# Two graph attention layers on one core: each mask turned over by one transposing transfer instead of four

## The chip, the cores and the metric

The kernel runs on one core of a Trainium2 chip. The metric is the device time of one execution in microseconds (us); lower is better. The kernel before takes 3692.95 us, the median of 3 runs from 3692.69 to 3693.4. A core has five engines that each work through a queue of their own: TensorE (PE, with its weight loads PEld), VectorE (DVE), ScalarE (ACT), GpSimd (POOL) and SyncE (SP), which here only issues transfers (DMA).

## What is computed

There are 32 graphs ("images") of 512 nodes with 512 features each, in float32, and an integer adjacency matrix per graph. Two attention layers run one after the other, each with a residual:

```python
# layer 0: scores along the rows of the adjacency, softmax over the last axis
h = jnp.maximum(_layernorm(x, axis=-1), 0.0)
scores = leaky_relu(s_src[:, :, None] + s_dst[:, None, :] + attn_b[0], 0.2)
attn = softmax(where(adj + eye == 0, -inf, scores), axis=-1)
x = x + einsum('bij,bjh->bih', attn, h)
# layer 1: two GAT layers, the first with 4 heads of 256 features, the second with 1 head of 512
h = jnp.maximum(_layernorm(x, axis=-1), 0.0)
mask = (adj > 0) | eye
#   gat_layer: xl = x @ W ; e[s, d] = leaky_relu(asrc[s] + adst[d], 0.2)
#              attn = softmax(where(mask, e, NEG_INF), axis=1) ; out = einsum(attn, xl) + bias
h = elu(gat_layer(h, mask, W1, ..., concat=True))
x = x + gat_layer(h, mask, W2, ..., concat=False)
```

Each softmax needs the mask twice: along one axis, to find the largest score of every node before the exponent is taken, and along the other, to be added to the score matrix. The adjacency isn't symmetric, so each mask is needed as it lies and turned over.

## The kernel before

**Tiling.** The 512 nodes of an image are `T = 4` tiles of `P = 128` partitions. A mask is a bf16 buffer of 128 x 4 x 512: `m[p, t, n]` is the entry of node `t*128 + p` (row) and node `n` (column), 0 where there is an edge and a large negative number where there is none. `m0` is the mask of layer 0, `m1` that of layer 1; `m0T` and `m1T` are the same masks turned over. There is one buffer each for `m0`, `m0T` and `m1T`, and two for `m1`.

**How a mask is made.** `load_adj` (L663) loads the adjacency by a GpSimd transfer that also converts it. For `m0`, VectorE adds the identity to the four diagonal blocks (L680) and maps to 0 and `NO_EDGE` (L683); for `m1` it maps first (L695) and then clears the diagonal blocks (L701). Then `transposed_mask` (L665 to L671) issues four transposing transfers on SP, one for each `t`. Each turns the 128 x 512 slab `m[:, t, :]` and writes the 128 columns `t*128 ... t*128+127` of all four tiles of `mT`.

**Who reads the masks.** `edge_weights` (L582) makes the softmax weights `E` of one head:

- `a_row`, a score for each node, is brought to all partitions: `in_lines` writes the scores of a layer to a small DRAM buffer (L559), `row_of` reads one line of it into all 128 partitions (L569, by SP), and `in_bank` copies the line to PSUM on ACT (L579).
- four instructions on VectorE (L591) add mask and row and keep the maximum, one for each tile. They read `m0` in layer 0 and `m1T` in layer 1 (`mask_max`).
- L596 and L598 make the largest score of each node, and `spread` brings it to a PSUM bank, `m_bank`, by four transposes on PE (L487).
- for each tile: ACT makes the raw scores from `c_row` (L609), VectorE subtracts `m_bank` (L612), GpSimd adds the mask (L614; `m0T` in layer 0, `m1` in layer 1), ACT takes the exponent (L617).

PE then multiplies `E` with the node values (`aggregate`, L627). There are six such passes for an image: one in layer 0, four heads and the single head of the last layer (the kinds `E_one` and `E`). The other big user of PE is `products` (L822), the projections `x @ W1` and `x @ W2`. There are 24 L591 and 24 L614 in an image, of them 20 L591 on `m1T` and 4 L614 on `m0T`.

**What sets the order.** Nothing is issued as it is written down. Each call of `op(...)` gives a planner the engine that can do an instruction, its cost and the buffers that it reads and writes. `Plan.run` makes up to six drafts of the whole program. In a draft each engine always takes the waiting operation that is due first; the due times of the next draft are worked back from the one before, and the best draft is issued. For a transfer the costs are the time on the issuing queue, the time until it lands, and the time that it holds the DMA engines. If one cost is changed, the order of instructions on all engines can change, and it is then fixed: an engine that waits for one instruction doesn't go on to the next. The costs of a transposing transfer are 2200, 3000 and 600 ns. The same planner gives out the buffer places.

Some lines that the steps of the prediction name and that lie in other functions: L378 is a score product on VectorE (for the first image also the products that prepare the second layer's weights), L471 a sum of weights on GpSimd, L493 to L502 are the layer norm, L645 adds an attention's result to `x`.

Of the kernel before, what the change touches and what calls it, by code (L numbers as in the profile page):

```python
# [12 lines left out]
ALU = mybir.AluOpType  # L13
PSUM = bass.MemoryType.PSUM

P = 128
# [4 lines left out]
LOWEST = -3.0e38  # L21
# [21 lines left out]
class Plan:  # L43
# [15 lines left out]
    def op(self, engines, cost, emit, reads=(), writes=(), ahead=0, lock=None):  # L59

        i = len(self.ops)
        after = set()
        for buf, part in reads:
            after.update(buf.wrote.get(part, ()))
        for buf, part in writes:
            after.update(buf.wrote.get(part, ()))
            after.update(buf.read.get(part, ()))
        bufs = []  # L70
        for buf, part in (*reads, *writes):
            if buf.kind is not None and buf not in bufs:
                bufs.append(buf)
                if not buf.ops and buf.kind in self.turns:
                    self.turns[buf.kind].append(buf)
                buf.ops.append(i)
        for buf, part in reads:
            buf.read.setdefault(part, []).append(i)
        for buf, part in writes:
            buf.wrote[part] = [i]  # L80
            buf.read[part] = []
        after.discard(i)
        if not isinstance(engines, tuple):
            engines, cost, emit = (engines,), (cost,), (emit,)
        self.ops.append((engines, cost, emit, after, bufs, i - ahead, lock))
# [153 lines left out]
def on_dve(n, speed=1.0, scaled_psum=False):  # L239
    one = n / 0.96 / speed + (130.0 if scaled_psum else 70.0)  # L240
    return one, one + 85.0


def on_act(n, per_partition=0):

    one = n / 1.2 + (95.0, 140.0, 280.0)[per_partition]
    return one, one + 60.0


def on_pool(n, narrow=False):  # L250
    one = 2.04 * n + 70.0 if narrow else 2.2 * n + 100.0
    return one, one + 30.0
# [8 lines left out]
def kernel(  # L261
# [24 lines left out]
    nc = tc.nc  # L286
    B, N, D = x.shape
    H, F = att_src1.shape
    HF = H * F
    T = N // P  # L290
# [18 lines left out]
    def node_block(t: int) -> slice:  # L309
        return slice(t * P, (t + 1) * P)  # L310
# [31 lines left out]
    junk = big.tile([P, 512], BF16, name="junk")  # L342
# [4 lines left out]
    op = plan.op  # L347
# [135 lines left out]
    ROW = range(T)  # L483
# [48 lines left out]
    def spread(kind, part, col_of, ahead):  # L532

        row = Buffer(kind)
        for t in range(T):
            pe_transpose(
                ahead, row, lambda t=t: row.at[:, node_block(t)], part, lambda t=t: col_of(t).to_broadcast([P, P]), ident, t
            )
        return row
# [24 lines left out]
    def row_of(kind, lines, k):  # L564

        row = Buffer(kind)
        op(
            "SP", by_dma(4 * P * N, 4500.0),
            lambda: nc.sync.dma_start(  # L569
                row.at, bass.AP(tensor=lines.at.tensor, offset=lines.at.offset + k * N, ap=[[0, P], [1, N]])  # L570
            ),
            lines(0), row(*ROW), AHEAD,
        )
        return row

    def in_bank(kind, row):

        bank = Buffer(kind)
        op("ACT", on_act(N), lambda: nc.scalar.copy(bank.at, row.at), row(*ROW), bank(*ROW), AHEAD)  # L579
        return bank  # L580

    def edge_weights(kind, scores, ac, lines, k, mask_max, mask):  # L582


        a_of = lambda t: ac.at[:, k, t : t + 1]
        a_row = spread("a_bank", scores, a_of, AHEAD) if lines is None else in_bank("a_bank", row_of("a_row", lines, k))
        amax, z, m = Buffer("col"), Buffer("col"), Buffer("col")
        for t in range(T):
            op(
                "DVE", on_dve(N + 60),  # L590
                lambda t=t: nc.vector.tensor_tensor_reduce(  # L591
                    junk, mask_max.at[:, t, :], a_row.at, 1.0, LOWEST, ALU.add, ALU.max, accum_out=amax.at[:, t : t + 1]
                ),
                a_row(*ROW) + mask_max(*ROW), amax(t),
            )
        op("DVE", on_dve(T), lambda: nc.vector.tensor_add(z.at, ac.at[:, k + 1, :], amax.at), scores + amax(*ROW), z(0))  # L596
        op(
            "DVE", on_dve(T), lambda: nc.vector.scalar_tensor_tensor(m.at, z.at, SLOPE, z.at, op0=ALU.mult, op1=ALU.max),  # L598
            z(0), m(0),
        )  # L600

        E = Buffer(kind)
        m_row = spread("m_bank", m(0) + E("place"), lambda t: m.at[:, t : t + 1], AHEAD)
        c_of = lambda t: ac.at[:, k + 1, t : t + 1]
        c_row = spread("acc", scores + E("place"), c_of, AHEAD) if lines is None else row_of("c_row", lines, k + 1)
        for t in range(T):
            op(
                "ACT", on_act(N, 1),
                lambda t=t: nc.scalar.activation(E.at[:, t, :], c_row.at, AF.Prelu, bias=a_of(t), scale=1.0, alpha=SLOPE),  # L609
                c_row(*ROW) + scores, E(t),  # L610
            )
            op("DVE", on_dve(N), lambda t=t: nc.vector.tensor_sub(E.at[:, t, :], E.at[:, t, :], m_row.at), m_row(*ROW) + E(t), E(t))  # L612
            op(
                "POOL", on_pool(N, True), lambda t=t: nc.gpsimd.tensor_add(E.at[:, t, :], E.at[:, t, :], mask.at[:, t, :]),  # L614
                E(t) + mask(*ROW), E(t), lock=True,
            )
            op("ACT", on_act(N), lambda t=t: nc.scalar.activation(E.at[:, t, :], E.at[:, t, :], AF.Exp), E(t), E(t))  # L617
        return E
# [44 lines left out]
        op("POOL", (2200.0, 8000.0), lambda: nc.gpsimd.dma_start(m.at, node_tiles(adj, b)), (), m(*ROW))  # L663

    def transposed_mask(m, mT):  # L665
        for t in range(T):
            op(
                "SP", (2200.0, 3000.0, 600.0),
                lambda t=t: nc.sync.dma_start(mT.at[:, :, node_block(t)], m.at[:, t, :], transpose=True),
                m(t), mT(t),  # L670
            )  # L671

    def masks0(b):

# [33 lines left out]
    def layer0_scores(b):  # L708
        rstd, nmr = layernorm(X[b])
        h0, ac = Buffer("h"), Buffer("ac")  # L710
        for t in range(T):
            relu_normed(h0, X[b], t, rstd, nmr)
            for i, w in ((1, ws_r), (0, wd_r)):
                op(
                    "DVE", on_dve(D), lambda t=t, w=w, i=i: dot(h0.at[:, t, :D], w, ac.at[:, i, t : t + 1]),
                    h0(t) + W["w0"](0, 1), ac((i, t)), lock=True,
                )
        c = ac(*((1, t) for t in ROW))
        op(
            "DVE", on_dve(T), lambda: nc.vector.tensor_scalar(ac.at[:, 1, :], ac.at[:, 1, :], b0_r, None, op0=ALU.add),  # L720
            c + W["w0"](2), c,
        )
        m0, m0T = masks0(b)
        scores = c + ac(*((0, t) for t in ROW))

        L0[b] = (h0, edge_weights("E_one", scores, ac, in_lines(ac, scores, 2) if b else None, 0, m0, m0T))
# [144 lines left out]
    def layer1_scores(b, h):  # L871
        xl, j = L1[b][h // 2], h % 2
        m1, m1T = M[b]
        if j == 0:
            ac = gather(
                xl(*((i, t) for t in range(T) for i in range(2))),
                lambda: xl_of(xl)[:, :, :, :2].rearrange("p t j i -> p j i t"), lambda: ac.at.rearrange("p (j i) t -> p j i t", j=2),
            )
            AC[b] = (ac, in_lines(ac, ac(0), 4))
        ac, lines = AC[b]  # L880
        return edge_weights("E", ac(0), ac, lines, 2 * j, m1T, m1)
# [44 lines left out]
    def layer2_project(b):  # L926
        h1T = H1T.pop(b)
        L1.pop(b)
        m1, m1T = M.pop(b)

        xl = Buffer("xl2" if b < B - 1 else "pair")
        if b == B - 1:
            op("POOL", (110.0, 120.0), lambda: nc.gpsimd.memset(xl2_of(xl)[:, :, 2 + D :], 1.0), (), xl(2))

        def dst(i, j, r, c):
            t = i * (T // 2) + r
            return xl((j, t)), lambda: xl2_of(xl)[:, t, j * W2 : (j + 1) * W2]

        products(
            lambda i, j: h1T_of(h1T[j])[:, :, i * HN : (i + 1) * HN],  # L940
            lambda i, j, g: h1T[j](*((2 * g + k, i) for k in range(2))),
            PER, weights_of("w2", KINDS_2), W2, range(1), lambda w, k, c: w2_s[w][:, k, :], dst, [xl],
        )
        ac = gather(
            xl(*((0, t) for t in range(T))), lambda: xl2_of(xl)[:, :, :2].rearrange("p t i -> p i t"), lambda: ac.at[:, :2, :]
        )
        L2[b] = (edge_weights("E_one", ac(0), ac, in_lines(ac, ac(0), 2) if b < B - 1 else None, 0, m1T, m1), xl)
# [85 lines left out]
```

## Time and profile before

| What | Value |
|---|---|
| time, median of 3 | 3692.95 us |
| span of the profiled execution | 3692.5 us |
| instructions | 51317 |
| granted TensorE clock, mean | 0.996 |
| L627 products on `pair,E` (4096 instructions) | 961.6 us busy |
| L591 on `m1T`, 640 instructions | 436.0 us busy, 681 ns each |
| L614 on `m`, kind `E`, 512 instructions | 620.2 us busy, 1240 ns each |
| transposing transfers on SP | 128 of `m0T`, 128 of `m1T`; median 4.2 and 2.4 us from issue to landing |
| transfer of a row, `a_row` (190) and `c_row` (190) | median 3.4 and 3.5 us from issue to landing |

The profile page gives each engine's busy time and its share of the span, the chain of work that ended last, and groups of instructions with the same line, engine, operation and tile, with the mean time of one and the idle time ahead of them. The trace behind it can be asked for a stretch of time, for waits (who waited for whom, total in us, how often, the longest) and for instructions in order of time. Each product of float32 operands shows as two PE instructions. In lines in order of time the first number is the start, the second the time, both in us; `x2` means that two instructions in a row were put together, and the time in brackets is idle time ahead of them. SPq marks an issue on the SP queue.

### The profile page before, as it was taken

Reading aid. Unit: us, or ns where it says so; the run is one execution under the profiler, and the core shown is the slowest. Engines: PE = TensorE matmul, PEld = TensorE weight load, DVE = VectorE, ACT = ScalarE, POOL = GpSimd, SP = SyncE. Lnnn points to the kernel's source line nnn. Section 1 sums busy time; section 2 is a strip of 40 time slices with the busy share of each in tenths; the row PEclk is TensorE's granted clock in tenths of the full one; section 3 lists DMA queues with packets and bytes.
Section 4 is the critical chain, followed back from the end, with each engine's and each line's share of the span. In section 5 each row is a group of like instructions: output and inputs, shape, how many; then the busy total and the mean of one; then the engine's idle time right before and its main releaser. Section 6 shows DMA issues by size and latency. Waiting matters only on the chain.

```text
span 3692.5 us, 51317 instructions
## 1 busy us (share of the span) xinstructions
PE 3625.2 (98%) x17806; PEld 3131.3 (85%) x17806; DVE 2878.2 (78%) x7478; ACT 1760.2 (48%) x3227; POOL 1592.1 (43%) x1353
## 2 busy tenths in 40 slices
PE   5899999999999999999999999999999999999998
PEld 4788888888888888888888888888888888888887
DVE  7988778877788877788877878777887778787755
ACT  2455444554454554445544445544455544455433
POOL 3534444534444444445344444444444444444332
PEclk9999999999999999999999999999999999999999
DMA  6244322334323333223333233442233422334310
GB/s 162 52 92 103 87 73 82 81 92 104 72 74 90 75 103 91 70 83 80 91 103 72 76 88 75 103 98 68 81 82 85 103 72 78 86 75 103 90 51 32
DMA packets 304342, 312.17 MB, mean 85 GB/s; under 512 B 150496, under 2 KB 188880, under 8 KB 304080
## 3 DMA queue, kind: packets, MB, share of 16 engines
q1 hardware_dynamic: 270288, 275.32, 26.2%
q0 software_dynamic: 33792, 33.56, 6.5%
q8 instruction: 140, 2.29, 0.3%
q14 instruction: 122, 1.00, 0.1%
HBM read 240.91 MB, written 67.89 MB: 84 GB/s over the span
## 4 chain that ended last, share of the span: by engine, by line
PE 94%; DVE 3%; DMA 1%; POOL 0%; issue 0%; ACT 0%; DVEq 0%; ACTq 0%
PE acc L627 46%; PE acc L822 41%; PE acc L487 4%; PE m_bank L487 2%; DVE junk L591 1%; DVE junk L378 0%; PE acc L553 0%; DVE E L612 0%; DMA m<-in_adj_dram 0%; DVE v L905 0%; POOL E_one L614 0%; DVE E_one L612 0%; DMA x<-in_x_dram 0%; DVE v L893 0%; DMA out_dram<-x 0%
## 5 line engine op out<-in xcount | busy, mean ns | idle before, releaser
L614 POOL TENSOR_TENSOR E<-E,m 128x512 f32<-128x512 f32 x512 | 620.2, 1240 | 803.3 <-DVE E L612 798.3
L627 PE MATMUL acc<-pair,E 128*128 128x257 f32 x4096 | 961.6, 381 | 1.4 <-ACT E L617 1.2
L627 PEld LDWEIGHTS acc<-pair,E 128*128 128x128 f32 x4096 | 743.0, 190 | 114.5 <-ACT E L617 14.4
L822 PE MATMUL acc<-w_T,E 128*128 128x257 f32 (+1 forms) x2048 | 521.5, 381 | 1.0 <-ACT pair L522 0.6
L627 PE MATMUL acc<-h,E_one 128*128 128x256 f32 (+1 forms) x2048 | 478.2, 382 | 6.3 <-ACT E_one L617 6.3
L617 ACT ACTIVATE E<-E 128x512 f32<-128x512 f32 x512 | 312.0, 624 | 315.4 <-POOL E L614 315.4
L627 PE MATMUL acc<-xl,E_one 128*128 128x257 f32 x1984 | 448.2, 379 | 0.0
L591 DVE CUSTOM_DVE_ANT_0 junk<-m1T,a_bank 128x512 bf16<-128x512 bf16 x640 | 436.0, 681 | 15.4 <-PE a_bank L487 1.7
L627 PEld LDWEIGHTS acc<-h,E_one 128*128 128x128 f32 x2048 | 383.8, 191 | 59.4 <-ACT E_one L617 7.6
L822 PEld LDWEIGHTS acc<-w_T,E 128*128 128x128 f32 x2048 | 379.6, 190 | 55.4 <-ACT pair L522 0.8
L627 PEld LDWEIGHTS acc<-xl,E_one 128*128 128x128 f32 x1984 | 371.4, 190 | 53.7
L612 DVE TENSOR_TENSOR E<-E,m_bank 128x512 f32<-128x512 f32 x512 | 326.5, 679 | 24.7 <-PE m_bank L487 24.7
L609 ACT ACTIVATE E<-c_row,ac 128x512 f32<-128x512 f32 x512 | 335.6, 708 | 1.9 <-DMA c_row<-lines 1.9
L520 ACT COPY pair<-acc 128x258 f32<-128x258 f32 (+1 forms) x375 | 138.2, 369 | 412.1 <-PE acc L822 410.3
L520 ACT COPY xl<-acc 128x257 f32<-128x257 f32 x219 | 81.7, 373 | 455.8 <-PE acc L822 455.8
L902 ACT ACTIVATE e<-v,minus_one 128x512 f32<-128x512 f32 x256 | 184.3, 720 | 236.4 <-DVE r L639 111.1
L645 DVE SCALAR_TENSOR_TENSOR x<-acc,r,x 128x256 f32<-128x256 f32 x512 | 240.6, 478 | 47.8 <-PE acc L627 43.6
L663 POOL DMA_DIRECT2D m<-in_adj_dram x64 | 51.4, 804 | 521.1 <-DVE col L591 476.8
L835 DVE TENSOR_TENSOR pair<-acc,pair 128x258 f32<-128x258 f32 (+1 forms) x390 | 164.5, 424 | 137.8 <-PE acc L822 127.7
L822 PE MATMUL acc<-w,hT 128*128 128x258 f32 x1024 | 268.4, 382 | 0.0
L822 PE MATMUL acc<-w,pair 128*128 128x257 f32 x1024 | 259.3, 380 | 0.0
L614 POOL TENSOR_TENSOR E_one<-E_one,m 128x512 f32<-128x512 f32 x128 | 145.0, 1165 | 263.2 <-DVE E_one L612 263.2
(108 smaller groups left out, 6117.7 us busy)
## 6 DMA issues: line engine op xcount, KB each, us to landing
a_row<-lines SPq DMA_DIRECT2D x190, 256.0 KB, 3.4
c_row<-lines SPq DMA_DIRECT2D x190, 256.0 KB, 3.5
x<-in_x_dram SPq DMA_DIRECT2D x32, 1024.0 KB
m<-in_adj_dram POOLq DMA_DIRECT2D x64, 512.0 KB, 7.0
spill<-x SPq DMA_DIRECT2D x32, 1024.0 KB, 4.3
x<-spill SPq DMA_DIRECT2D x32, 1024.0 KB
out_dram<-x SPq DMA_DIRECT2D x30, 1024.0 KB, 5.0
m0T<-m SPq DMA_TRANSPOSE x128, 4.2
```

What stands on the lines that cost most here:

```text
L487: op("PE", on_pe(P, transpose=True), lambda: nc.tensor.transpose(dst_of(), src_of(), identity), src, dst(part), ahead)
L520: nc.scalar.copy(dst_of(), src_of())
L591: lambda t=t: nc.vector.tensor_tensor_reduce(junk, mask_max.at[:, t, :], a_row.at, 1.0, LOWEST, ALU.add, ALU.max, accum_out=amax.at[:, t : ...
L609: lambda t=t: nc.scalar.activation(E.at[:, t, :], c_row.at, AF.Prelu, bias=a_of(t), scale=1.0, alpha=SLOPE),
L612: op("DVE", on_dve(N), lambda t=t: nc.vector.tensor_sub(E.at[:, t, :], E.at[:, t, :], m_row.at), m_row(*ROW) + E(t), E(t))
L614: "POOL", on_pool(N, True), lambda t=t: nc.gpsimd.tensor_add(E.at[:, t, :], E.at[:, t, :], mask.at[:, t, :]),
L617: op("ACT", on_act(N), lambda t=t: nc.scalar.activation(E.at[:, t, :], E.at[:, t, :], AF.Exp), E(t), E(t))
L627: lambda s=s: nc.tensor.matmul(acc.at[:, :n], E.at[:, s, node_block(t)], of(s), start=(s == 0), stop=(s == T - 1)),
L645: lambda acc=acc, r=r, f=f, t=t: nc.vector.scalar_tensor_tensor(X.at[:, t, f], acc.at[:, :HD], r.at, X.at[:, t, f], op0=ALU.mult, op1=ALU. ...
L822: lambda k=k: nc.tensor.matmul(acc.at[:, :width], at[a]()[:, k, node_block(r)], weight_of(w, k, c), start=(first and k == 0), stop=(k == n ...
L835: op("DVE", on_dve(width), lambda: nc.vector.tensor_add(place(), acc.at[:, :width], place()), acc(0) + token, token)
L902: op("ACT", on_act(2 * F, 1), lambda e=e, ts=ts: nc.scalar.activation(e.at, v.at[:, ts, :], AF.Exp, bias=minus_one), parts, e(0))
```

## The change

A mask is turned over by one transposing transfer. Source and destination are seen as rows of 16 blocks of 128: source block `t*4 + a` is the block of rows `t` and columns `a`, and the same block of the destination holds it turned over. The destination is therefore kept block by block: `mT[p, t, a*128 + n]` where it was `mT[p, a, t*128 + n]`. The readers take this into account: `mask_row(mask, t)` picks, for a turned mask, block `t` of each of the four slabs, which gives the same 512 entries in the same order as before, in four runs of 128 that lie 512 entries apart. Their other operands are seen as 4 x 128 as well (`by_blocks`). The planner is given other costs for the transfer: 4000 ns on the queue, 2000 until it lands, 4000 on the DMA engines. It has 64 transfers of this kind to place where it had 256.

```diff
 # edge_weights
-                    junk, mask_max.at[:, t, :], a_row.at, 1.0, LOWEST, ALU.add, ALU.max, accum_out=amax.at[:, t : t + 1]
+                    by_blocks(junk), mask_row(mask_max, t), by_blocks(a_row.at), 1.0, LOWEST, ALU.add, ALU.max, accum_out=amax.at[:, t : t + 1]
...
-                "POOL", on_pool(N, True), lambda t=t: nc.gpsimd.tensor_add(E.at[:, t, :], E.at[:, t, :], mask.at[:, t, :]),
+                "POOL", on_pool(N, True), lambda t=t: nc.gpsimd.tensor_add(by_blocks(E.at[:, t, :]), by_blocks(E.at[:, t, :]), mask_row(mask, t)),
...
     def transposed_mask(m, mT):
-        for t in range(T):
-            op(
-                "SP", (2200.0, 3000.0, 600.0),
-                lambda t=t: nc.sync.dma_start(mT.at[:, :, node_block(t)], m.at[:, t, :], transpose=True),
-                m(t), mT(t),
-            )
+        op(
+            "SP", (TURN, 2000.0, TURN),
+            lambda: nc.sync.dma_start(
+                mT.at.rearrange("p a (b n) -> p (a b) n", n=P), m.at.rearrange("p t n -> p (t n)"), transpose=True
+            ),
+            m(*ROW), mT(*ROW),
+        )
+
+    TURN = 4000.0
+
+    def by_blocks(row):
+        return row.rearrange("p (b n) -> p b n", n=P)
+
+    def mask_row(mask, t):
+        if mask.kind in ("m0T", "m1T"):
+            return mask.at.rearrange("p a (b n) -> p a b n", n=P)[:, :, t, :]
+        return by_blocks(mask.at[:, t, :])
```

## The prediction, made before the changed kernel was run

> **What bounds the kernel now.** I read the page's busy shares and its chain first, then the busy time by stretch, then TensorE's waits, then the transfer queue in one image of the steady stretch.
>
> ```profile
> PE 3625.2 (98%) x17806; PEld 3131.3 (85%) x17806; DVE 2878.2 (78%) x7478; ACT 1760.2 (48%) x3227; POOL 1592.1 (43%) x1353
> PE 94%; DVE 3%; DMA 1%; POOL 0%; issue 0%; ACT 0%; DVEq 0%; ACTq 0%
> ```
>
> TensorE is busy 98% of the span and carries 94% of the chain that ended last. Idle are 3692.5 - 3625.2 = 67 us. By stretch (the first column after the window's length is PE's busy time; after the engines come clock, DMA share, GB/s):
>
> ```profile
> 0.00:50.00 50.00, 16.44 (x59) 12.88 (x60) 32.31 (x96) 9.15 (x13) 13.75 (x21) 1.00 0.92 236
> 50.00:100.00 50.00, 35.12 (x154) 29.24 (x154) 47.43 (x132) 17.76 (x38) 20.47 (x13) 0.87 0.35 88
> 100.00:162.00 62.00, 56.45 (x260) 46.94 (x260) 57.74 (x161) 31.96 (x53) 32.46 (x25) 0.94 0.15 32
> 500.00:612.00 112.00, 112.00 (x554) 96.94 (x554) 88.01 (x228) 54.59 (x100) 49.41 (x42) 1.00 0.33 85
> 3643.00:3693.00 50.00, 40.33 (x180) 33.98 (x178) 15.74 (x36) 8.44 (x17) 6.26 (x5) 0.91 0.06 22
> ```
>
> In the steady stretch PE is busy for 112.00 of 112.00 us: nothing can be won there, only lost. The idle time lies in the start (33.6 + 14.9 + 5.6 us in the first three rows) and in the end (9.7). PE's waits up to 500 us:
>
> ```profile
> PE a_bank L487 <- DVE junk L378: 26.7, 4, 25.2
> PE m_bank L487 <- DVE col L598: 13.1, 5, 5.1
> PE acc L487 <- ACT h L510: 7.0, 1, 7.0
> PE acc L627 <- ACT E_one L617: 6.3, 3, 2.7
> ```
>
> None of them names a transfer. The changed transfers in one steady image, in the SP queue:
>
> ```profile
> 1555.34 2.54 SPq L669 DMA_TRANSPOSE m1T<-m  x2
> 1557.92 1.34 SPq L559 DMA_DIRECT2D lines<-e  x1
> 1559.31 2.50 SPq L669 DMA_TRANSPOSE m1T<-m  x2
> 1561.90 0.53 SPq L569 DMA_DIRECT2D a_row<-lines  x1
> 1562.47 0.43 SPq L569 DMA_DIRECT2D c_row<-lines  x1
> 1563.00 2.52 SPq L669 DMA_TRANSPOSE m0T<-m  x2
> 1567.97 0.32 SPq L559 DMA_DIRECT2D lines<-e  x1
> 1568.33 1.19 SPq L669 DMA_TRANSPOSE m0T<-m  x1
> 1569.63 0.52 SPq L569 DMA_DIRECT2D a_row<-lines  x1
> 1570.19 1.21 SPq L669 DMA_TRANSPOSE m0T<-m  x1
> ```
>
> Each quarter turn holds SP for 1.2 us, and row transfers slip in between the quarters.
>
> **What the Trainium skill says.** "DMA: Bandwidth & Descriptors", section "Latency and other measured facts", gives a DMA transpose 261 GB/s, or about 350 to 400 where contiguous: for a mask of 128 x 2048 x 2 B = 0.52 MB an estimate of 1.3 to 2.0 us. The trace agrees with the slow end: from 85.3 to 90.4 us, with four turns and little else, the DMA share was 0.40, so 0.40 x 5.1 = 2.0 us of all 16 engines. The turn is limited by its issue, not by moving. The same page, "Issuing engines are not separate DMA queues": transfers of all engines share the 16 DMA engines and interleave. The trace agrees: quarter turns alone landed after 2.4 us, and one issued at 1564.3, beside GpSimd's mask load, after 8.2. "TensorE: Matmul & The Clock Gate", section "What's actually happening": an idle window of about 3.4 us halves the clock. The trace agrees: after the 7.0 us wait the granted clock was 0.50 from 60 to 65 us. "SBUF — State Buffer", section "SBUF: two separate sides": VectorE and GpSimd lock each other out of a shared port pair. The trace agrees: an L680 beside GpSimd's L471 took 2.00 us, elsewhere 0.29.
>
> **The change part by part.** *Turns.* 256 quarters become 64 wholes. No row shows a whole. The lower bound of its SP time is one quarter, 1.2 us, if the cost is per instruction; the upper bound is 4 x 1.2 = 4.8, if it is per block. I take 4.8, as the start's quarters held SP longer on busy DMA engines (6.62 for four), which speaks for a cost by content. Landing comes 2.4 us after the issue ends. m1T is first read by L591 at 1569.39, 14 us after its turn starts, and m0T most of an image later: both stay hidden.
>
> *Reads by blocks.* 768 L591 (681 ns on m1T, 684 on m) and 640 L614 (1240, 1165, and 1156 on m0T) read the same elements, with runs of 128 that stay contiguous. Zero, bounded above by 0.1 us each. VectorE has 112.0 - 88.0 = 24 us idle per image and GpSimd 63, which hide 24 and 20 such instructions.
>
> *Order.* The planner has new costs, so every engine's order moves. I compared the two issue orders. In the steady image PE's order is the same up to L627 on xl,E_one; then the first head's m_bank comes 3 products later, 3 x 2 x 0.217 = 1.3 us, while the first pair,E product keeps its place. The last 60 rows of PE and VectorE are alike, so the tail keeps its 9.7 us.
>
> *Steady row transfers.* SP's order is now m1T, lines, m0T, a_row, c_row. So a_row is issued at 1555.34 + 4.8 + 0.35 + 4.8 + 0.1 = 1565.4 instead of 1561.90. It is queued behind m0T, and behind it wait in turn ACT's L579, L591, L598, m_bank, L612, L614, L617, PE. Its landing takes 3.4 us (page) to 8.2 (the turn beside the mask load); I take 3.9, as measured for the a_row issued at 1569.63 beside that load: 1569.3. L579 ran at 1567.85 because of ACT's own order, so it is 1.45 us later; L591 starts at 1569.9 instead of 1569.39, L598 ends near 1574.0, and m_bank is due only at 1574.85 + 1.3 = 1576.15. VectorE now has one L591 and one L645 of later work ahead of L612: it gets there at 1574.0 + 1.5 (the work between L598 and L612 before) + 0.7 + 0.4 = 1576.6, and m_bank is written at 1576.75. From there 0.6 (L612) + 0.2 + 1.15 (L614) + 0.65 (L617) give an E at 1579.35; PE wants it at 1579.61. **Nothing is lost, with 0.3 us to spare.**
>
> *Start.* (a) The scale L502 stands behind the second mask (landed at 20.8) instead of ahead of it, so the score products L378 start at 22.9, not 22.0; a mask load of 0.8 us stands ahead of the first L614. PE's first attention starts some 0.8 us late. (b) For the second image's E_one, 16 instead of 6 of the second layer's L378 (0.465 us each) stand ahead of L591: 4.7 us. With (a) and small shifts m_bank comes at 101.3, not 95.74, and PE starts again at 105.2, not 99.60. (c) Those 10 products are missing later. The first head's L598 comes near 109.2 instead of 111.1; PE works on E_one until 119, the 0.59 and 3.01 us of waits at 116.7 and 127.8 vanish, and so does the clock of 0.76 from 125 to 132. At the third head's m_bank I count +1.1 us. The waits after it (0.79 + 0.59 + 0.34 + 0.56 = 2.3 us) can take up more. Net -1 to +2; I take +1.
>
> Sum: 3692.95 + 1 + 0 = **3694 us**.
>
> **The rivals.** *Forecast (0.57): hidden.* 3690 to 3699.
>
> *Slower (0.33): the row waits behind the whole turn.* For it: the turns stand together ahead of a_row, and GpSimd's mask load (issued at 1564.03, 8.1 us to land) now lies exactly over a_row's transfer. Against: SP may issue a whole faster than 4.8. Only 0.4 us more than my 3.9 are free (0.3 of slack and rounding); with 5.2 us to land PE waits 0.9 us in each of some 30 steady images: 3694 + 27 = 3721. With 8.2 it would be 3.9 x 30 = 117, the far end, which I give little weight, since the a_row beside the same load took 3.9.
>
> *Faster (0.10): the start gets shorter.* PE waits 13.6 us after 91 us (5.14 + 2.54 + 0.59 + 3.01 + 2.3), partly at half clock. If the new order loses 9 of them, 3684. Against: the first two waits grow by (b).
>
> **Numbers.** The range reaches from the faster case to the middle of the slower one and a little beyond: 3684 to 3726. It leaves out some 0.05 below and 0.12 above. Of the forecast's share nearly all lies within 7.4 us (0.2%), a few hundredths of the slower case too: faster 0.09, same 0.59, slower 0.32.
>
> **What would show it.** Right: 64 turns of 4 to 5 us on SP; PE's busy time again equal to the window from 500 to 612; L591 and L614 within 2% per instruction; m_bank of the second image's E_one near 101 us, and no wait of 3 us near 128. Wrong: a wait of PE on ACT's E at L627 in every image, with a_row landing over 4.3 us after its issue; a turn of 1.2 us, which leaves the row early; or a slower L591 or L614.

## The result, and the profile after

The changed kernel takes 3719.58 us, the median of 3 runs from 3718.58 to 3720.66. The ratio to the kernel before is 1.0072, with a 95% interval from 1.0049 to 1.0095: it is slower by 26.6 us. The two profiled executions are 24.3 us apart (spans 3716.8 and 3692.5). From L680 of the kernel before on, line numbers are 13 higher in the changed one: L822 is now L835, L835 is L848, L890 is L903, L893 is L906, L902 is L915 and L905 is L918. The last four finish a head on VectorE and ACT: L903 and L906 scale its result and add the bias, which gives `v`; L915 takes the exponent of `v` and L918 joins the two. TensorE then transposes `v` (L487 on `acc` from `v`).

The page of the changed kernel, busy shares and chain by engine:

```profile
PE 3642.3 (98%) x17806; PEld 3134.2 (84%) x17806; DVE 2843.6 (77%) x7452; ACT 1767.0 (48%) x3253; POOL 1585.9 (43%) x1353
PE 73%; DVE 19%; ACT 4%; POOL 2%; issue 1%; DMA 0%; DVEq 0%; ACTq 0%; POOLq 0%
```

TensorE still looks busy for 98% of the span, but only 73% of the chain that ended last is its own (94% before), and 19% is VectorE's. Transfers have almost no part in it: DMA has 0%. The same windows as before show where (columns as in the prediction: length, then busy time and number of instructions of PE, PEld, DVE, ACT and POOL):

```profile
500.00:612.00 112.00, 111.70 (x551) 96.25 (x550) 86.13 (x227) 54.72 (x101) 48.80 (x42) 1.00 0.32 85
1200.00:2000.00 800.00, 797.89 (x3917) 687.65 (x3916) 611.94 (x1604) 384.69 (x709) 345.28 (x294) 1.00 0.32 84
```

The same 800 us of the kernel before:

```profile
1200.00:2000.00 800.00, 800.00 (x3950) 692.53 (x3949) 627.68 (x1631) 387.96 (x713) 348.85 (x297) 1.00 0.33 85
```

The busy time hides most of the loss; the number of instructions doesn't. TensorE got through 3917 instructions instead of 3950. Over the whole stretch from 388 to 3400 us it is 14744 instead of 14870; 126 instructions at 112.0 / 554.5 = 0.202 us are about 25.4 us. Up to 388 us the changed kernel is ahead, with 1575 instructions to 1566 (about 1.8 us). So the loss lies in the steady images alone: 25.4 - 1.8 = 23.6 of the 24.3 us. One image takes 113.57 us instead of 112.62 (from the spill issued at 508.03 to the one at 848.74, three images on; before from 509.08 to 846.93).

The waits of the weight loads (PEld), which run ahead of the products, from 500 to 3400 us; first after, then before:

```profile
PEld acc L627 <- ACT E L617: 37.3, 75, 0.6
```

```profile
PEld acc L627 <- ACT E L617: 9.6, 53, 0.2
```

75 waits are three in each of 25 images: TensorE is there before the exponent L617 of a head's E. Before there were two small ones. One steady image, first of the changed kernel, then of the kernel before (start, time, and in brackets the wait and its releaser):

```profile
1595.11 1.17 PEld L627 LDWEIGHTS acc<-pair,E 128*128 128x128 f32 x6 [0.38 <-ACT E L617]
1596.86 2.03 PEld L627 LDWEIGHTS acc<-pair,E 128*128 128x128 f32 x10 [0.58 <-ACT E L617]
1616.78 0.30 PEld L627 LDWEIGHTS acc<-pair,E 128*128 128x128 f32 x2 [0.53 <-ACT E L617]
```

```profile
1580.43 2.05 PEld L627 LDWEIGHTS acc<-pair,E 128*128 128x128 f32 x10 [0.20 <-ACT E L617]
1608.06 0.73 PEld L627 LDWEIGHTS acc<-pair,E 128*128 128x128 f32 x4 [0.17 <-ACT E L617]
```

Of the three of the changed kernel, the first two stand at the first and second tile of the second head, the third at the fourth head; the first head has none.

**Is it the transfer?** The SP queue of the same image:

```profile
1562.90 1.79 SPq L669 DMA_TRANSPOSE m1T<-m  x1
1565.41 0.45 SPq L559 DMA_DIRECT2D lines<-e  x1
1565.95 2.94 SPq L669 DMA_TRANSPOSE m0T<-m  x1
1568.99 0.53 SPq L569 DMA_DIRECT2D a_row<-lines  x1
1569.57 0.42 SPq L569 DMA_DIRECT2D c_row<-lines  x1
```

A whole turn holds SP for 1.8 to 3.2 us (medians from 500 to 3400 us: 1.86 for `m1T`, 2.01 for `m0T`; the 2.94 of this image is one of the longer ones), not 4.8. To compare with the image of the kernel before, 7.56 us are to be taken off: L627's first product on `xl,E_one` starts at 1571.90 here and at 1564.34 there. So a_row is issued at 1561.43 on the clock of before, 0.5 us *earlier* than there (1561.90), although it stands behind `m0T`. Over 154 rows ACT's L579 waited for its transfer once, 0.3 us. The a_row is not late.

Another row is waited for: the c_row of the second head, in front of its first L609. The view of c_row from 500 to 3400 us, who waited for it (us, times):

```profile
  ACT E L609: 31.0, 26
```

That is 1.2 us in each image, and the kernel before has no such wait. But this row is issued at 1578.51, 9.6 us after the last turn has left SP, and the wait isn't passed on to TensorE: behind these L609 ACT is idle for 3.25 us until GpSimd releases the first head's L617. The run dve_swap below has the same wait (31.0 us) and lacks most of the loss.

**Is it the order?** The second head on VectorE, from its largest score (L598) to L612:

```profile
1589.96 0.14 DVE L598 SCALAR_TENSOR_TENSOR col<-col 128x4 f32<-128x4 f32 x1
...
1590.42 0.67 DVE L591 CUSTOM_DVE_ANT_0 junk<-m1T,a_bank 128x512 bf16<-128x512 bf16 x1
...
1591.13 0.69 DVE L591 CUSTOM_DVE_ANT_0 junk<-m1T,a_bank 128x512 bf16<-128x512 bf16 x1
...
1591.87 0.69 DVE L591 CUSTOM_DVE_ANT_0 junk<-m1T,a_bank 128x512 bf16<-128x512 bf16 x1
...
1592.48 1.28 DVE L612 TENSOR_TENSOR E<-E,m_bank 128x512 f32<-128x512 f32 x2
```

TensorE's four transposes for this head's m_bank, and the same with L612 in the kernel before:

```profile
1591.07 0.60 PE L487 MATMUL m_bank<-ident,col 128*128 128x128 f32 x4
```

```profile
1582.72 0.60 PE L487 MATMUL m_bank<-ident,col 128*128 128x128 f32 x4
1583.52 1.87 DVE L612 TENSOR_TENSOR E<-E,m_bank 128x512 f32<-128x512 f32 x3
```

The transposes end at 1591.67, but L612 starts at 1592.48: in the order three L591 of the *third* head stand ahead of it, the last from 1591.87. Before, L612 of the second head began at 1583.52, 0.2 us after its m_bank. On one clock it is 1592.48 - 7.56 - 1583.52 = 1.40 us later: 0.79 because m_bank itself has a later place on TensorE (1591.07 against 1582.72), 0.61 because of the L591. On ACT, the exponents of that head:

```profile
1594.43 0.63 ACT L617 ACTIVATE E<-E 128x512 f32<-128x512 f32 x1 [4.15 <-POOL E L614]
1594.97 1.32 ACT L609 ACTIVATE E<-c_row,ac 128x512 f32<-128x512 f32 x2
1596.19 0.61 ACT L617 ACTIVATE E<-E 128x512 f32<-128x512 f32 x1
```

Two L609 of the third head stand between the first and the second L617. It is there that the second wait, of 0.58 us, is seen; what takes it away is tried below.

### The profile page after: what moved, and what is told of

The parts are those of the page before. It is cut to its first block, busy times and chain, and to the rows that moved or that the text cites. A ratio compares the mean times of both kernels' runs of the same rounds, so it can differ in the third digit from the quotient of the medians.

```text
span 3716.8 us, 50892 instructions
## 1 busy us (share of the span) xinstructions
PE 3642.3 (98%) x17806; PEld 3134.2 (84%) x17806; DVE 2843.6 (77%) x7452; ACT 1767.0 (48%) x3253; POOL 1585.9 (43%) x1353
## 4 chain that ended last, share of the span: by engine, by line
PE 73%; DVE 19%; ACT 4%; POOL 2%; issue 1%; DMA 0%; DVEq 0%; ACTq 0%; POOLq 0%
PE acc L835 42%; PE acc L627 27%; DVE E L612 5%; DVE junk L591 5%; PE acc L487 3%; POOL E L614 2%; ACT E L617 2%; DVE v L906 2%; DVE v L918 1%; DVE st L493 1%; ACT E L609 1%; PE m_bank L487 1%; DVE x L645 1%; ACT e L915 1%; DVE col L596 1%
## 5 line engine op out<-in xcount | busy, mean ns | idle before, releaser
L627 PE MATMUL acc<-pair,E 128*128 128x257 f32 x4096 | 980.7, 383 | 9.0 <-ACT E L617 4.8
L614 POOL TENSOR_TENSOR E<-E,m 128x512 f32<-128x512 f32 x512 | 607.9, 1216 | 851.2 <-DVE E L612 849.6
L627 PEld LDWEIGHTS acc<-pair,E 128*128 128x128 f32 x4096 | 747.4, 190 | 136.5 <-ACT E L617 42.8
L835 PE MATMUL acc<-w_T,E 128*128 128x257 f32 (+1 forms) x2048 | 522.1, 381 | 0.1
L627 PE MATMUL acc<-h,E_one 128*128 128x256 f32 (+1 forms) x2048 | 487.6, 382 | 6.0 <-ACT E_one L617 6.0
L617 ACT ACTIVATE E<-E 128x512 f32<-128x512 f32 x512 | 317.8, 621 | 318.2 <-POOL E L614 316.3
L627 PE MATMUL acc<-xl,E_one 128*128 128x257 f32 x1984 | 448.5, 379 | 0.0
L591 DVE CUSTOM_DVE_ANT_0 junk<-m1T,a_bank 128x512 bf16<-128x512 bf16 x640 | 435.5, 680 | 14.7 <-PE a_bank L487 1.7
L627 PEld LDWEIGHTS acc<-h,E_one 128*128 128x128 f32 x2048 | 383.5, 191 | 58.6 <-ACT E_one L617 6.8
L835 PEld LDWEIGHTS acc<-w_T,E 128*128 128x128 f32 x2048 | 379.4, 190 | 54.0 <-ACT pair L522 0.5
L627 PEld LDWEIGHTS acc<-xl,E_one 128*128 128x128 f32 x1984 | 371.1, 190 | 53.9 <-ACT E_one L617 0.2
L609 ACT ACTIVATE E<-c_row,ac 128x512 f32<-128x512 f32 x512 | 341.9, 708 | 41.1 <-DMA c_row<-lines 40.8
L612 DVE TENSOR_TENSOR E<-E,m_bank 128x512 f32<-128x512 f32 x512 | 328.3, 679 | 11.7 <-PE m_bank L487 11.6
L915 ACT ACTIVATE e<-v,minus_one 128x512 f32<-128x512 f32 x256 | 183.0, 715 | 209.5 <-DVE v L906 202.9
L835 PE MATMUL acc<-w,hT 128*128 128x258 f32 x1024 | 268.6, 382 | 0.7 <-DVE pair L848 0.6
L918 DVE SCALAR_TENSOR_TENSOR v<-e,v 128x512 f32<-128x512 f32 x256 | 219.1, 856 | 65.4 <-ACT e L915 63.5
L848 DVE TENSOR_TENSOR pair<-acc,pair 128x258 f32<-128x258 f32 (+1 forms) x390 | 164.4, 424 | 131.3 <-PE acc L835 123.5
L614 POOL TENSOR_TENSOR E_one<-E_one,m 128x512 f32<-128x512 f32 x128 | 144.3, 1160 | 268.9 <-DVE E_one L612 268.9
```

The lines of the kernel that those rows point to most:

```text
L591: lambda t=t: nc.vector.tensor_tensor_reduce(by_blocks(junk), mask_row(mask_max, t), by_blocks(a_row.at), 1.0, LOWEST, ALU.add, ALU.max, a ...
L614: "POOL", on_pool(N, True), lambda t=t: nc.gpsimd.tensor_add(by_blocks(E.at[:, t, :]), by_blocks(E.at[:, t, :]), mask_row(mask, t)),
L627: lambda s=s: nc.tensor.matmul(acc.at[:, :n], E.at[:, s, node_block(t)], of(s), start=(s == 0), stop=(s == T - 1)),
L835: lambda k=k: nc.tensor.matmul(acc.at[:, :width], at[a]()[:, k, node_block(r)], weight_of(w, k, c), start=(first and k == 0), stop=(k == n ...
L848: op("DVE", on_dve(width), lambda: nc.vector.tensor_add(place(), acc.at[:, :width], place()), acc(0) + token, token)
L915: op("ACT", on_act(2 * F, 1), lambda e=e, ts=ts: nc.scalar.activation(e.at, v.at[:, ts, :], AF.Exp, bias=minus_one), parts, e(0))
```

## The experiments

Two theories. **A**: the planner's new prices changed the order on all engines, and that order costs the time (the buffer places go with it; they weren't tried apart); whole turns and reads by blocks cost nothing. **B**: the transfer costs it, since a row waits behind a whole turn or beside it. B is the rival of the prediction that came near the time. Times are medians; each ratio is to runs of the kernel before on the same chip, with its 95% interval. Where a kernel has added lines, its line numbers are a few higher.

### old_order_whole: the order of before, the whole turn

```diff
-        op(
-            "SP", (TURN, 2000.0, TURN),
...
-            m(*ROW), mT(*ROW),
-        )
+        left = list(range(T))
+
+        def turn():
+            left.pop()
+            if not left:
+                nc.sync.dma_start(
+                    mT.at.rearrange("p a (b n) -> p (a b) n", n=P), m.at.rearrange("p t n -> p (t n)"), transpose=True
+                )
+
+        for t in range(T):
+            op("SP", (2200.0, 3000.0, 600.0), turn, m(t), mT(t))
```

> The planner is given the four quarter turns with the costs of the kernel before, so all engines have the order of the kernel before; but the first three quarters issue nothing and the fourth issues the whole turn. Masks are kept and read block by block. Theory A (the order is the cause: in the changed order the chain m_bank, L612, L614, L617 of a head comes about 1.3 us later and PE waits at the second head and later; whole turns and reads by blocks cost nothing): 3693, from 3690 to 3695, PE busy for 112.0 of the 112 us from 500 to 612. Theory B (the transfer is the cause: a row waits behind the whole turn or beside it): 3705 to 3720, with PE waits on ACT E L617 in each image.

Measured: 3692.85 us, ratio 1.0001 (0.9993 to 1.0009). Its window in the steady stretch:

```profile
500.00:612.00 112.00, 112.00 (x555) 96.81 (x554) 88.59 (x230) 54.56 (x100) 48.85 (x43) 1.00 0.33 85
```

TensorE is full. The a_row stands directly behind the whole turn of `m1T` in this order. This kernel has every part of the change that runs on the chip, the whole turns and all reads by blocks, and none of the loss. Theory A gave this number, B is out by 12 us or more. It is also what the change is worth in the old order: nothing, as the turns were hidden.

### new_order_quarters: the new order, four quarter turns

```diff
+        def turn():
+            for t in range(T):
+                nc.sync.dma_start(mT.at[:, t, :].rearrange("p (a n) -> p a n", n=P), m.at[:, t, :], transpose=True)
+
-        op(
-            "SP", (TURN, 2000.0, TURN),
...
-            m(*ROW), mT(*ROW),
-        )
+        op("SP", (TURN, 2000.0, TURN), turn, m(*ROW), mT(*ROW))
```

> The order of the changed kernel on all engines (one planner operation with its costs), but this operation issues four quarter turns in a row instead of the whole. The layout by blocks stays. It puts a price on the turn's time on SP: about 5 us for four quarters instead of the 1.8 to 2.9 us that the whole took. First a_row of the image then issued about 4.4 us later, ACT's L579 some 1.9 us later. Theory A: the loss of the order stays (27 us) and 1.6 us in each of 27 images come on top: about 3764, at least 3745. Theory B: the same direction, but as much as the SP time says, 4 us an image: 3820. If the turn's time on SP does not matter at all: 3720.

Measured: 3789.06 us, ratio 1.0262 (1.0248 to 1.0276), 69.5 us more than the changed kernel. In its SP queue the two turns of this image together hold SP for 11.5 us (in the median of all images 5.13 each); then L579's idle time, by what ended it, and the waits of the weight loads, both from 500 to 3400 us:

```profile
1591.91 5.87 SPq L669 DMA_TRANSPOSE m1T<-m  x4
1597.82 0.58 SPq L559 DMA_DIRECT2D lines<-e  x1
1598.50 5.63 SPq L669 DMA_TRANSPOSE m0T<-m  x4
1604.23 0.53 SPq L569 DMA_DIRECT2D a_row<-lines  x1
```

```profile
  DMA a_row<-lines: 113.7, 44
```

```profile
PEld acc L627 <- ACT E L617: 79.4, 100, 1.9
PEld m_bank L487 <- DVE col L598: 23.5, 25, 2.2
```

a_row is issued 12.3 us after the first turn starts, with whole turns 6.1 (medians of all images 11.1 and 5.2). ACT then really waits for it: for the first head's row 3.72, 5.22, 4.07 and 4.26 us in four images one after another, and mostly for the next row too, some 0.5 us. TensorE's weight loads wait (79.4 - 37.3 + 23.5) / 25 = 2.6 us more in each image than in the changed kernel, and 69.5 us in 27 images are 2.6 us too. My 3764 was too low because I had the first row 4.4 us later and 1.6 us of it lost; it is 5.9 us later in the median. So the mechanism of B exists, and shows as a wait of L579 on the transfer; in the changed kernel it isn't there, because the whole turn is short. In the new order the whole turn saves 69 us, in the old one nothing.

### measured_cost and turn3000: other prices, the same turn

```diff
 # measured_cost
-            "SP", (TURN, 2000.0, TURN),
+            "SP", (1900.0, 2400.0, 2000.0),
 # turn3000
-    TURN = 4000.0
+    TURN = 3000.0
```

> The changed kernel with one edit: the planner's costs of the whole turn are 1900, 2400 and 2000 ns (near what the trace shows) instead of 4000, 2000 and 4000. All engines get another order. Theory A: the time moves with the order; with the first head's row planned earlier the stall at the second head goes: 3694, but any value from 3688 to 3712 as the order is new. Theory B (the transfer itself): the transfer is the same, so 3715 to 3725.

> The changed kernel with the planner's price of the turn at 3000 instead of 4000 ns (on the queue and on the DMA engines). All engines get another order once more. Theory A: the time follows the order that comes out and not the transfer; with the first row planned some 1 us earlier the steady stretch should be full or nearly: 3696, from 3688 to 3715. Theory B: 3719.

Measured: 3697.5 us (ratio 1.0014, 1.0007 to 1.0020) and 3720.85 us (1.0075, 1.0063 to 1.0088). With the measured price TensorE is full from 500 to 612 us (112.00 of 112.00): the waits at L627 are down to 5.9 us. In the profiled execution, 1.1 us longer than that of the kernel before (spans 3693.6 and 3692.5), what is left lies in the start, where up to 388 us TensorE did 329.7 us of work against 331.2 before; the medians are 5 us apart, and where the rest lies is open. With the price 3000, the waits at L627 are gone altogether, but each image has another one:

```profile
1597.30 0.14 PEld L487 LDWEIGHTS acc<-ident,v 128*128 128x128 f32 x1 [1.50 <-DVE v L918]
```

The transposes of the first head's result wait for VectorE's L918. My 3696 was wrong here: 3000 is nearer to the measured hold than 4000 and the time is no better. Theory B is out by 17 us for measured_cost; its 3719 for turn3000 fits the time, but by chance: the wait there is on VectorE's L918 and not on a row.

### quarters_cost1250: the price alone, without the change

```diff
 # the kernel before
-                "SP", (2200.0, 3000.0, 600.0),
+                "SP", (1250.0, 2400.0, 600.0),
```

> A control without any part of the change on the chip: the kernel before with its four quarter turns, its layout and its reads, where only the planner's price of a quarter turn is what the trace shows (1250 ns on the queue and 2400 to landing instead of 2200 and 3000). Theory A (the price alone, through the order, moves the time by this much, whatever the turn): another time than before by more than 2 us, anywhere from 3680 to 3725. Rival: the order hardly depends on the price of the quarter, and the time stays at 3692 to 3694.

Measured: 3713.26 us, ratio 1.0055 (1.0042 to 1.0069). Quarter turns, the old layout, the old reads: only the price is another, and 21 us are lost. Two of its waits in one image:

```profile
1580.74 0.41 PEld L487 LDWEIGHTS m_bank<-ident,col 128*128 128x128 f32 x4 [0.90 <-DVE col L598]
1587.50 1.60 PEld L627 LDWEIGHTS acc<-pair,E 128*128 128x128 f32 x8 [0.46 <-ACT E L617]
```

So an edit of a price, with no other turn and no other read, can by itself cost as much as was to be explained.

### Moves by hand in the changed kernel

Each moves a few instructions in the planner's finished order, in every image; the transfers stay. `raws`, `subs`, `exps` and `tops` are the numbers of a head's L609, L612, L617 and L591, one for each tile; 1 and 2 mark the second and the third head. The first edit stands where the planner issues its best draft (a pair `(i, behind)` puts instruction `i` directly behind `behind`), the others name what is moved behind what; act_behind does the same with the second tile's exponent, `exps1[1]`, in place of `exps1[3]`.

```diff
+        for i, behind in self.moves:
+            at = best.order.index(behind)
+            if i in best.order[:at]:
+                best.order.remove(i)
+                best.order.insert(at, i)
         for i in best.order:
...
 # dve_swap
+                plan.moves += [(tops2[2], subs1[1])]
 # act_all
+                plan.moves += [(raws2[1], exps1[3]), (raws2[0], exps1[3])]
 # dve_act: both
```

> The changed kernel with two ACT instructions of each image moved in the order: the first two L609 of the third head go behind the second L617 of the second head, in front of which they stood. Nothing else moves. Theory A: the wait of PE before the second head's second tile (0.58 us in each image) goes, the 0.38 us before its first tile stays: about 3704. Theory B: no change, 3718 to 3721.

Measured: 3732.92 us (ratio 1.0110, 1.0096 to 1.0124), worse by 13. ACT and PEld of that image (L627 is L617 here, L637 is L627, L618 is L609):

```profile
1601.81 0.63 ACT L627 ACTIVATE E<-E 128x512 f32<-128x512 f32 x1 [0.49 <-POOL E L623]
1602.35 1.32 ACT L618 ACTIVATE E<-c_row,ac 128x512 f32<-128x512 f32 x2
...
1604.19 0.61 ACT L627 ACTIVATE E<-E 128x512 f32<-128x512 f32 x1
...
1604.85 0.73 PEld L637 LDWEIGHTS acc<-pair,E 128*128 128x128 f32 x4 [1.01 <-ACT E L627]
```

The wait at the second tile is gone; the pair and an L915 now stand ahead of the third L617, and there PE waits 1.01 us. I had not asked what comes next in the queue.

> The changed kernel with one instruction of VectorE moved in each image: the third L591 of the third head goes behind the first two L612 of the second head, ahead of which it stood. L612 then starts at m_bank plus little, some 0.65 us earlier. Theory A (PE waits because the second head's chain m_bank, L612, L614, L617 is late by the order): both waits at the second head (0.38 and 0.58 us an image) all but go, the one at the fourth head stays: 3697, from 3694 to 3704. Theory B (something in the transfer): 3718 to 3721.

Measured: 3703.20 us, ratio 1.0028 (1.0017 to 1.0039). One instruction of VectorE, moved by two places, gives back 16.4 of the 26.6 us. The two waits left in an image (L639 is L627, L629 is L617, and L918 is L906 here):

```profile
1592.17 2.46 PEld L639 LDWEIGHTS acc<-pair,E 128*128 128x128 f32 x12 [0.22 <-DVE v L918]
1612.53 0.30 PEld L639 LDWEIGHTS acc<-pair,E 128*128 128x128 f32 x2 [0.53 <-ACT E L629]
```

As theory A had it, both waits of the second head on L617 are gone (0.22 us on another instruction came in), and the one at the fourth head stays. It is 6 us above my 3697: I had not put the remaining waits against those of the kernel before, and not counted the new one.

> The changed kernel with the first two L609 of the third head moved behind all four L617 of the second head on ACT (in the earlier trial they went behind the second alone and PE waited 1.0 us for the third instead). Theory A: the wait at the second tile goes, that at the first (0.38) stays, the second L915 is some 1.3 us later and may cost 0.3: 3706, from 3700 to 3715. If ACT's order is not the cause: 3719.

> Both moves together. Theory A: 3697, from 3693 to 3704, no better than the VectorE move alone if that already takes both waits away.

Measured: 3734.59 us (1.0112, 1.0098 to 1.0126) and 3727.90 us (1.0094, 1.0079 to 1.0109). Both are misses of mine. The waits of act_all from 500 to 3400 us (L639 is L627, L493 is L487; L930 is L918, the result's last step on VectorE, and L918 is L906):

```profile
PEld acc L639 <- ACT E L629: 29.9, 50, 0.8
PEld acc L493 <- DVE v L930: 20.9, 50, 0.6
PEld acc L493 <- DVE v L918: 4.7, 25, 0.2
```

The pair of L609, moved behind, now stands ahead of an L915, and the transposes of the result wait for the L918 that needs it: 20.9 us that the changed kernel doesn't have. That the pair alone causes all of them is my reading of the order and wasn't tried. In this order the L609 is where the wait could be *seen*, and moving it cost more than it gave; the move upstream, on VectorE, took the wait away.

The last move is made in turn3000: there the first L918 of the first head goes behind the L915 that it needs.

```diff
             e = Buffer("e")
+            if h == half == 0:
+                plan.moves.append((len(plan.ops) + 1, len(plan.ops)))
```

> The order of the kernel with the price 3000 has one wait in each image, 1.50 us of the weight loads for the transposes of the first head's result (L487 on acc from v, on VectorE's L918), and a start that is some 2.6 us of TensorE work ahead. The edit: the first L918 of the first head goes directly behind the exponent L915 that it needs, ahead of L598 and two L906, five places earlier on VectorE. Theory A: the wait goes and nothing takes its place: 3720.9 - 27 x 1.5 = 3680, from 3677 to 3695, and so faster than the kernel before. Rival: the L906 that are now later hold up TensorE elsewhere and half of the gain is lost: 3700. The whole turn is the same in all of these.

Measured: 3720.12 us, ratio 1.0074 (1.0061 to 1.0086), no gain at all: a miss, and worse than the rival's 3700. The one wait of 1.50 us has become four in each image (L491 is L487, L631 is L627, L924 is L918, L621 is L617):

```profile
1595.99 0.14 PEld L491 LDWEIGHTS acc<-ident,v 128*128 128x128 f32 x1 [0.90 <-DVE v L924]
1602.14 0.73 PEld L631 LDWEIGHTS acc<-pair,E 128*128 128x128 f32 x4 [0.24 <-ACT E L621]
1603.27 1.60 PEld L631 LDWEIGHTS acc<-pair,E 128*128 128x128 f32 x8 [0.40 <-ACT E L621]
1605.16 0.42 PEld L491 LDWEIGHTS acc<-ident,v 128*128 128x128 f32 x4 [0.30 <-DVE v L924]
```

### two_prices: a good start and a full steady stretch

```diff
-            "SP", (TURN, 2000.0, TURN),
+            "SP", (3000.0, 2000.0, 3000.0) if b < 4 else (1900.0, 2400.0, 2000.0),
```

> The changed kernel with two prices of the whole turn: 3000, 2000, 3000 ns for the first four images, whose order then is that of the kernel with the price 3000 up to about 250 us (a start with 4 us more of TensorE work done by 388 us than with the measured price), and 1900, 2400, 2000 from there on, whose steady images have no wait. Theory A (time is the start's and the steady stretch's order added up): 3697.5 - 4 to 6 = 3692, from 3687 to 3697. If the two orders do not join without a new wait: 3700 or more.

Measured: 3690.17 us, ratio 0.9993 (0.9985 to 1.0002). The median is the lowest of all kernels here, 29 us under the changed one with the same transfers, but it can't be told from the kernel before. Start and steady stretch:

```profile
162.00:388.00 226.00, 224.84 (x1109) 193.64 (x1108) 188.72 (x475) 115.98 (x212) 106.02 (x91) 1.00 0.35 87
500.00:612.00 112.00, 112.00 (x554) 96.99 (x552) 87.81 (x229) 54.57 (x102) 46.83 (x42) 1.00 0.32 85
```

The start brings 51.52 + 57.12 + 224.84 = 333.5 us of TensorE work by 388 us (331.2 before). From 388 to 3400 us TensorE waits only three times, 2.5 us in all, for L598 ahead of an m_bank. Of the price 3000's 3720.85 only the start was kept, of the measured price's 3697.5 only the steady images.

| Kernel | Turn | Order | us |
|---|---|---|---|
| before | quarters | of before | 3692.95 |
| old_order_whole | whole | of before | 3692.85 |
| after | whole | price 4000 | 3719.58 |
| new_order_quarters | quarters | price 4000 | 3789.06 |
| dve_swap | whole | price 4000, one L591 moved | 3703.20 |
| act_behind | whole | price 4000, two L609 moved | 3732.92 |
| act_all | whole | price 4000, two L609 moved further | 3734.59 |
| dve_act | whole | price 4000, both moves | 3727.90 |
| turn3000 | whole | price 3000 | 3720.85 |
| turn3000_l918 | whole | price 3000, one L918 moved | 3720.12 |
| measured_cost | whole | price 1900 | 3697.50 |
| quarters_cost1250 | quarters | quarter at 1250 | 3713.26 |
| two_prices | whole | 3000, then 1900 | 3690.17 |

## Where the prediction was right and where it was wrong

The forecast was 3694, the time is 3719.58. It lies in the range, but in the part that was kept for the rival "the row waits behind the whole turn". That rival put a wait of 0.9 us into 30 images and had 3721. That it comes so near is luck: its row was never late. The range holds the time only because it was drawn to take in the middle of that rival; the forecast itself, that nothing is lost, is wrong by 26 us.

- **Bound.** Right. A full steady stretch can only lose, and the whole loss lies there.
- **Turns.** Wrong. I took 4.8 us on SP for a whole, because four quarters at the start had held SP longer on busy DMA engines. It is 1.86 and 2.01 in the median, nearer to the lower bound of 1.2. The 1.3 to 2.0 us that the prediction estimated from the Trainium skill ("DMA: Bandwidth & Descriptors", "Latency and other measured facts") for moving the mask lie nearer to the measured hold of a whole on SP; that the hold is the time of moving is not shown. My sentence that the turn is limited by its issue was read off quarters, and no run tests it for a whole.
- **Reads by blocks.** Right: L591 680 ns on `m1T` (681 before), 685 on `m` (684); L614 1149 on `m0T` (1156), 1160 on `E_one` with `m` (1165). On `E` it is 1216 (1240). I counted 640 L614; with those on `m0T` they are 768, which changes nothing at a price of zero.
- **First row.** Wrong by the same 4.8: not issued 3.5 us later, but 0.5 us earlier on the clock of before, in the image shown. The slack that I spent on it was never used up.
- **First head.** Right. m_bank is 1.29 us later (1583.70 - 7.56 - 1574.85; predicted 1.3), L612 1.23 later, and the first product on `pair,E` is on time to 0.01 us, with E ready 0.24 us ahead of it (predicted 0.3).
- **"Nothing is lost."** This is the step that failed. It followed one chain, that of the first head, compared the two orders as far as the first head's E, and put the heads after it at nothing without following them. The second head's m_bank has a later place too (0.79), L591 of the third head stands ahead of its L612 (0.61 more) and L609 ahead of its second L617 (dve_swap, which moves one of these L591 alone, takes both waits of the second head away and 16.4 of the 26.6 us). TensorE, which had come to the first head with 0.24 us to spare, had nothing to spare at the second and at the fourth. In one image the waits on L617 are 0.38 + 0.58 + 0.53 = 1.49 us; before they were 0.20 + 0.17. The difference of 1.1 us is near the 0.95 us by which an image is longer. At the fourth head the chain is not slower: the second E is ready 5.0 us after m_bank starts (1611.72 to 1616.73), before 5.3 (1602.70 to 1608.01). But TensorE has only 4.5 us of work between the two places in the new order, where it had 5.2. No run moved that; the wait stays in dve_swap.
- **Start.** The sign is wrong: predicted +1, the changed kernel is about 1.8 us ahead by 388 us. Four of its waits:

```profile
97.92 1.12 PE L487 MATMUL m_bank<-ident,col 128*128 128x128 f32 x4 [6.63 <-DVE col L598]
101.79 11.65 PE L627 MATMUL acc<-h,E_one 128*128 128x257 f32 x40 [2.75 <-ACT E_one L617]
133.85 0.89 PE L487 MATMUL acc<-ident,v 128*128 128x128 f32 x4 [3.04 <-DVE v L906]
151.22 3.31 PE L627 MATMUL acc<-pair,E 128*128 128x257 f32 x14 [0.88 <-DVE v L906]
```

  m_bank came at 97.92, not 101.3, and TensorE restarted at 101.79, not 105.2: of the shift of 5.6 us that I worked out in (b), 2.2 were there. The waits of 0.59 and 3.01 us did vanish (c), but one of 3.04 came at 133.85, on another line, that I hadn't counted.
- **Tail.** Right: waits of 2.7, 2.7 and 1.4 us after 3400 us (2.7, 2.7 and 1.3 before).

What would show it wrong was named correctly, a wait of PE on ACT's E at L627 in every image; but it was tied to a row that lands late, and the row did not.

What stays open: why the planner chose the late places as its best draft. The trace shows L609 at 0.71 us (0.64 back to back, 2.55 for four) where its price is 0.57, and L617 at 0.62 where it is 0.52. That its prices of ACT, and not those of the turn, are at fault wasn't tried.

## What to carry to other kernels

Where a planner or scheduler sets the order, a change to a transfer is two changes: keep the old order with the new transfer, and the new order with the old one, before either is blamed. When a full engine is fed by a chain that repeats (here one head after another), follow the new order through a whole period and not only to the first consumer: here the first had slack and the next ones had none. Look for the place where the lateness begins and not only for the one where the wait is seen: of the five moves by hand only the one of an L591 ahead of L612 gained, the three that moved L609 (one of them together with that L591) and the one of L918 did not.

## What the runs showed of the hardware

One transposing transfer of 128 x 2048 holds SP for 1.8 to 2.0 us when nothing is in its way, and one of 128 x 512 for 1.2: four times the content takes about one and a half times as long. Four quarters back to back take 5.13 us in the median of new_order_quarters and up to 6.45. Close to other transfers the hold of a whole was longer: the turn of `m0`, which in old_order_whole is issued straight behind the transfer of a row, takes 2.99 us in the median, and the first whole of the changed kernel, among the loads of the start, 7.6. Reads in four runs of 128 cost nothing against one run of 512: 680 ns against 681 for L591 on `m1T`, 1149 against 1156 for L614 on `m0T`.
